# Triangle stage: channel sums kept in PSUM, squares summed on GpSimd, product stores on SyncE's queue, and the output stage's first tiles asked for earlier

## The chip, the cores and the metric

The kernel runs on one core of one Trainium2 chip. A core has five engines that run side by side, each with its own queue of instructions: PE (TensorE, matmuls), DVE (VectorE), ACT (ScalarE), POOL (GpSimd) and SP (SyncE, which here only issues transfers). They meet through semaphores. Transfers between the device's DRAM and the on-chip memory SBUF are issued on a queue (here SP's or POOL's) and carried out by 16 DMA engines. Matmuls write PSUM[...]. The metric is the device time of one execution in microseconds, as the median over several runs.

## The reference

Four residual layers on an image of 256 x 256 pixels with 128 channels, in float32. The change lies in the third, a gated triangle product:

```python
def _L2_conv_ref(pair, ln_in_w, ln_in_b, p_in_w, g_in_w, ln_out_w, ln_out_b, p_out_w, g_out_w):
    pair_norm = layer_norm(pair, ln_in_w, ln_in_b)
    p = jnp.einsum('bijd,hd->bijh', pair_norm, p_in_w)
    g = jax.nn.sigmoid(jnp.einsum('bijd,hd->bijh', pair_norm, g_in_w))
    left = g[..., :H] * p[..., :H]
    right = g[..., H:] * p[..., H:]
    out = jnp.einsum('bikd,bjkd->bijd', left, right / jnp.float32(L))
    out = layer_norm(out, ln_out_w, ln_out_b)
    out = jnp.einsum('bijh,dh->bijd', out, p_out_w)
    gate = jax.nn.sigmoid(jnp.einsum('bijd,ed->bije', pair_norm, g_out_w))
    return gate * out

x = x + _L2_conv_ref(_gn(x), ...)      # third of four such lines
```

For each of the 128 channels `d` the product is a 256 x 256 matrix, left times the transpose of right. The second layer norm runs over the channels, so it needs, for each pixel, the sum over the 128 products and the sum of their squares.

## The kernel before

`triangle` has three parts, run one after the other.

The first part normalises the image in tiles of 2048 pixels, keeps the result in DRAM as `znT`, keeps the inverse roots of its variances as `rs2D`, and already fills `LR` for the first quarter of the channels. `LR` is a tile of 128 KB per partition that holds left and right for 32 channels.

The second part is a loop over the four quarters `g`. A **fill** (not for `g` = 0) goes through the pixels in 64 blocks `b`: SP fetches `zt` from `znT`, 1 MB for two blocks, into `X[0]` to `X[3]` in turn; PE computes `z`, the gate and the value for 8 groups of 128 pixels, into two banks of PSUM; ACT takes the sigmoid of its first half (`sg`); DVE multiplies into `LR`. A **product stage** then goes through the 32 channels `d`: PE computes `po`, a product, in one bank of a `z` tile; ACT copies it, reordered and scaled, into `o` (two instructions); `o` is stored as a row of `prodD`; DVE forms `df`, the product less the first product (`shift`); the channel sum `total` is increased by `df` on DVE; and one product later, `add_square` has ACT square `df` and adds the square on POOL to `even`, or for every fourth channel on DVE to `odd`. `shift`, `total`, `even` and `odd` are the four quarters of the fifth tile, `X[4]`.

After the last quarter the sums are joined, ACT takes Ln and Exp of the variance (which need one table of functions, the sigmoid needs another; `table` asks for one), and the inverse roots go to DRAM as `rs3D`. In between, `transformed_taps` (called as `prepare`) makes the last layer's weights `U` from small matmuls `cpk`, ACT copies `kw` and a dozen short DVE instructions; its instructions may be placed among the others.

The third part, the output stage, goes through the image again in 32 tiles of 2048 pixels, with an order of steps written out by hand in `order`: `lx` and `lp` fetch `x` and the products `pd`; `pa` and `pb` spread the inverse roots `ra` (from `rs2D`) and `rb` (from `rs3D`) over the partitions by matmul; `xs` and `sc` scale; `e0` and `e1` give the gate `pe`, `y0` and `y1` the projected product `py`; `gy`, `ad`, `qu` and `st` finish a tile and store it. `ra` and `rb` are fetched by `roots`, four transfers for four tiles. `x` and `pd` have five buffers each.

Instructions wrapped in `pin` keep the order of the program on their engine. The others, among them SP's fetches, are placed by a scheduler. Memory comes from pools: a new tile that lies where an old one lay waits for the old one's last users. The tiles of the output stage lie where `X`, `LR` and the work tiles lay. Two engines that read the same PSUM tile are kept one behind the other, so `df` waits for `o`.

Of the kernel before, what the change touches and what calls it, by code (L numbers as in the profile page):

```python
# [9 lines left out]
F32 = mybir.dt.float32  # L10
AF = mybir.ActivationFunctionType
ALU = mybir.AluOpType
# [19 lines left out]
class Kernel:  # L32
# [21 lines left out]
    def act(self, out, in_, func, bias=0.0, scale=1.0, **kw):  # L54
        return self.nc.scalar.activation(out, in_, func, bias=bias, scale=scale, **kw)  # L55
# [4 lines left out]
    def mm(self, out, lhsT, rhs, start=True, stop=True):  # L60
        return self.nc.tensor.matmul(out, lhsT, rhs, start=start, stop=stop)  # L61
# [1050 lines left out]
    def triangle(self, x2T, x3T, znT, prodD, rs2D, rs3D, stats2, shift2, stats3, shift3, prepare):  # L1112
# [12 lines left out]
        with ExitStack() as c:  # L1125
# [70 lines left out]
            with ExitStack() as c1:  # L1196
# [97 lines left out]
                io = c1.enter_context(self.pool(name="t2", bufs=3))  # L1294
                ps = c1.enter_context(self.pool(name="t2s", bufs=2, space=PSUM))
                table(SIGMOID)
                shift, total, even, odd = (X[4][:, k * 512:(k + 1) * 512] for k in range(4))
                nc.gpsimd.memset(X[4][:, 512:], 0.0)
                squared = []

                def add_square():
                    if squared:
                        n, t = squared.pop()
                        act(t, t, AF.Square)
                        if n % 4:
                            pin(nc.gpsimd.tensor_tensor)(even, even, t, ADD)
                        else:
                            tt(odd, odd, t, ADD)

                for g in range(G):  # L1310

                    for b in range(NB if g else 0):
                        if b % 2 == 0:
                            zt = X[b // 2 % 4]
                            nc.sync.dma_start(zt, znT[:, b * 1024:(b + 2) * 1024])
                        z = ps.tile([P, 8, P], F32, name="z", bufs=4)
                        for ch in range(8):
                            o = (b % 2) * 1024 + ch * P
                            mm(z[:, ch, :], zt[:, o:o + P], wf[:, g].rearrange("c t d -> c (t d)"))
                        sg = work.tile([P, 8, 2 * CQ], F32, name="sg")  # L1320
                        act(sg, z[:, :, :2 * CQ], AF.Sigmoid)
                        rows = lambda t: t.rearrange("p (x q) f -> p x q f", x=2)
                        tt(LR[:, :, :, :, 2 * b:2 * b + 2].rearrange("p a k f x -> p x (a k) f"),
                           rows(z[:, :, 2 * CQ:]), rows(sg), MUL)

                    for d in range(CQ):
                        po = ps.tile([P, 8, P], F32, name="z", bufs=4)[:, :4]
                        pa = po.rearrange("p (a b) j -> p a b j", a=2)
                        for a in range(2):
                            for kc in range(2):  # L1330
                                mm(pa[:, a], LR[:, a, kc, d, :], LR[:, :, kc, CQ + d, :], start=kc == 0, stop=kc == 1)
                        o = io.tile([P, 2, P, 2], F32, name="o")
                        for a in range(2):
                            act(o[:, a], pa[:, a].rearrange("p b j -> p j b"), AF.Copy, scale=1.0 / N)
                        nc.gpsimd.dma_start(prodD[g * CQ + d].rearrange("(p a j) -> p a j", p=P, a=2),  # L1335
                                            o.rearrange("p a j b -> p a (j b)"))
                        add_square()
                        if g + d == 0:
                            act(shift, po.rearrange("p k j -> p (k j)"), AF.Copy, scale=1.0 / N)
                        else:  # L1340
                            df = io.tile([P, 512], F32, name="df", bufs=3)
                            stt(df, po.rearrange("p k j -> p (k j)"), 1.0 / N, shift, MUL, ALU.subtract)
                            tt(total, total, df, ADD)
                            squared.append((g * CQ + d, df))

                add_square()
                tt(even, even, odd, ADD)
                stt(total, total, -1.0 / P, total, MUL, MUL)
                tt(even, even, total, ADD)
                table(LN_EXP)  # L1350
                act(even, even, AF.Ln, bias=self.eps, scale=1.0 / P)
                rsm = io.tile([P, 2, P, 2], F32, name="o")
                for a in range(2):
                    act(rsm[:, a], even.rearrange("p (a b j) -> p a b j", a=2, b=2)[:, a].rearrange("p b j -> p j b"), AF.Exp, scale=-0.5)
                nc.sync.dma_start(rs3D[0].rearrange("(p n) -> p n", p=P), rsm.rearrange("p a j b -> p (a j b)"))

            quarters.close()
            prepare(W["kt"], W["wd"], W["bv"])
# [2 lines left out]
            with ExitStack() as c1:  # L1361
# [3 lines left out]
                D = [{} for _ in range(M)]  # L1365
                half = lambda t, h: t[:, h * 1024:(h + 1) * 1024]
                R = {}
                table(SIGMOID)

                def roots(b, name, src, queue=nc.sync):  # L1370
                    if b * 4 < M:
# [24 lines left out]
                load_x, load_pd = load("x", x2T, 5), load("pd", prodD, 5)  # L1396

                def lx(d):
                    if d["p"] % 4 == 0:
                        roots(d["p"] // 4 + 1, "ra", rs2D)  # L1400
                    load_x(d)

                def lp(d):
                    if d["p"] % 4 == 2:
# [39 lines left out]

                def st(d): pin(nc.gpsimd.dma_start)(x3T[:, d["p"] * 2048:(d["p"] + 1) * 2048], d["x"])

                roots(0, "ra", rs2D)
                roots(0, "rb", rs3D, nc.gpsimd)
                order = (
                     (lx, 0), (pa, 0), (y0, 1), (y1, 1), (xs, 0), (lp, 0), (gy, 1), (e0, 0), (pb, 0), (ad, 1),  # L1450
# [290 lines left out]
```

## Time and profile before

The three runs took 4733.85, 4735.3 and 4738.4 us; the median is 4735.3.

| | |
|---|---|
| profiled execution, its own time | 4734.2 us |
| its span (first to last instruction) | 4732.1 us |
| busy share PE, DVE, ACT, POOL | 96%, 80%, 70%, 45% |
| mean granted clock of PE | 0.989 |
| first part of `triangle` ends, first product | 3270.6 us |
| product stages on PE, first product to next stage's start | 59.2, 60.6, 60.6, 60.4 us |
| fills (three), 1024 matmul records each | about 115 us each |
| last product ends on PE, first `py` of the output stage | 3863.1, 3898.9 us |
| output stage, last layer | to 4195, to 4732 us |

In a line of the timeline the columns are the start in us from the span's start, the length in us, the engine, the line of the kernel, the instruction with its output and inputs, shapes and count; the bracket tells how long the engine had been idle before and what ended that wait. Consecutive equal instructions are merged. A line that belongs to a helper (55, 61, 1119) stands for every caller, so tiles tell more than lines. Each float32 matmul of the program shows as two records. `X`'s tiles, `shift`, `total`, `even` and `odd` are all named `zt` in the profile, and `po` is named `z`. SPq and POOLq are the queues' own issue times. In the list of groups the columns after the first bar are busy time in us and mean ns of one, after the second idle time before the group and what ended it.

### The profile page before, as it was taken

Reading aid. Unit: us, or ns where it says so; the run is one execution under the profiler, and the core shown is the slowest. Engines: PE = TensorE matmul, PEld = TensorE weight load, DVE = VectorE, ACT = ScalarE, POOL = GpSimd, SP = SyncE. Lnnn points to the kernel's source line nnn. Section 1 sums busy time; section 2 is a strip of 40 time slices with the busy share of each in tenths; the row PEclk is TensorE's granted clock in tenths of the full one; section 3 lists DMA queues with packets and bytes.
Section 4 is the critical chain, followed back from the end, with each engine's and each line's share of the span. In section 5 each row is a group of like instructions: output and inputs, shape, how many; then the busy total and the mean of one; then the engine's idle time right before and its main releaser. Section 6 shows DMA issues by size and latency. Waiting matters only on the chain.

```text
span 4732.1 us, 79416 instructions
## 1 busy us (share of the span) xinstructions
PE 4533.6 (96%) x30421; PEld 2596.8 (55%) x30421; DVE 3791.8 (80%) x4847; ACT 3332.4 (70%) x5174; POOL 2139.1 (45%) x1457
## 2 busy tenths in 40 slices
PE   8999999999999999999999998799999979999999
PEld 2444555555555533333333333456989963379999
DVE  6776777777777689999999999687676677789885
ACT  6555888888888899999999999697344344442210
POOL 0343555555555557666766666334142145520000
PEclk9999999999999999999999999899999989999999
DMA  8893122222222235555555555665756739955332
GB/s 305 301 349 140 46 84 88 82 85 81 90 81 86 81 87 134 132 131 130 135 131 130 135 131 116 206 260 216 267 208 238 264 138 344 362 218 172 127 118 72
DMA packets 212969, 769.13 MB, mean 163 GB/s; under 512 B 58630, under 2 KB 61980, under 8 KB 172244
## 3 DMA queue, kind: packets, MB, share of 16 engines
q1 hardware_dynamic: 136286, 432.10, 27.5%
q0 software_dynamic: 75008, 331.54, 23.8%
q8 instruction: 243, 3.98, 0.3%
q14 instruction: 136, 1.11, 0.1%
q10 hardware_dynamic: 1296, 0.40, 0.0%
HBM read 431.26 MB, written 265.55 MB: 147 GB/s over the span
## 4 chain that ended last, share of the span: by engine, by line
PE 61%; ACT 16%; DVE 12%; issue 7%; DMA 2%; POOL 1%; SPq 0%; ACTq 0%; POOLq 0%; DVEq 0%
PE z L61 10%; PE m L61 8%; PE nd L61 7%; PE sc L61 6%; PE ppq L61 3%; PE ppv L61 3%; PE pe L61 2%; PE zc L61 2%; PE py L61 2%; PE ppg L61 2%; PE ppk L61 2%; PE px L61 2%; ACT L933 2%; PE pr L61 2%; ACT x2q L55 2%
## 5 line engine op out<-in xcount | busy, mean ns | idle before, releaser
L592 DVE TENSOR_TENSOR e<-sc,bT 128x1024 f32<-128x1024 f32 x512 | 613.1, 1219 | 256.1 <-PE sc L61 254.0
L592 POOL TENSOR_TENSOR ks<-e 128x1024 f32<-128x1024 f32 x256 | 601.6, 2370 | 442.7 <-PE nd L61 429.3
L55 ACT ACTIVATE e<-e 128x1024 f32<-128x1024 f32 x512 | 539.0, 1053 | 39.2 <-DVE e L592 29.6
L61 PE MATMUL m<-U,v 128*128 128x128 f32 x4608 | 514.8, 275 | 0.0
L61 PEld LDWEIGHTS m<-U,v 128*128 128x128 f32 x4608 | 514.6, 192 | 0.0
L61 PEld LDWEIGHTS z<-wf,zt 128*128 128x128 f32 x4096 | 462.8, 192 | 55.7 <-DVE LR L1119 27.4
L61 PE MATMUL z<-wf,zt 128*128 128x128 f32 x4096 | 475.5, 277 | 7.2 <-DVE LR L1119 4.9
L1119 DVE TENSOR_TENSOR LR<-z,sg 128x512 f32<-128x512 f32 (+1 forms) x320 | 268.3, 873 | 156.9 <-ACT sg L55 156.9
L55 ACT ACTIVATE sg<-z 128x512 f32<-128x512 f32 (+1 forms) x320 | 159.8, 512 | 233.7 <-PE z L61 230.2
L61 PE MATMUL sc<-proj 32*128 32x256 f32 x4096 | 299.9, 403 | 3.1 <-DVE e L592 2.2
L961 POOL TENSOR_TENSOR fs<-f 128x512 f32<-128x512 f32 x64 | 175.7, 2746 | 269.8 <-DVE f L958 250.2
L61 PEld LDWEIGHTS sc<-proj 32*128 32x128 f32 x4096 | 187.9, 185 | 160.8 <-PE px L61 94.8
L61 PE MATMUL nd<-e,proj 128*32 128x256 f32 x4096 | 272.3, 384 | 2.6 <-DVE og L592 2.6
L61 PE MATMUL z<-LR 128*128 128x256 f32 x1024 | 226.6, 381 | 21.4 <-DVE df L1119 15.1
L55 ACT ACTIVATE dn<-dn 128x512 f32<-128x512 f32 x384 | 237.9, 620 | 10.3 <-DVE dn L592 6.2
L961 POOL TENSOR_TENSOR u<-t,tr 128x512 f32<-128x512 f32 x64 | 235.3, 3677 | 11.8 <-DVE tr L964 10.6
L961 POOL TENSOR_TENSOR t<-t,v 128x1024 f32<-128x1024 f32 x64 | 210.2, 3284 | 57.3 <-DVE t L958 57.3
L1335 POOL DMA_DIRECT2D prodD<-o x128 | 70.7, 553 | 356.4 <-ACT o L55 352.9
L1626 POOL DMA_DIRECT2D out_dram<-ys x32 | 37.0, 1155 | 424.0 <-DVE ys L1624 412.1
L61 PEld LDWEIGHTS z<-LR 128*128 128x128 f32 x1024 | 192.5, 190 | 54.7 <-issue 21.0
L1616 ACT COPY m4s<-m 128x512 f32<-128x512 f32 x32 | 18.6, 583 | 287.3 <-PE m L61 287.3
L1119 POOL TENSOR_TENSOR x<-ga,x 128x1024 f32<-128x1024 f32 x62 | 144.6, 2347 | 135.6 <-DVE ga L1119 135.6
(408 smaller groups left out, 10920.8 us busy)
## 6 DMA issues: line engine op xcount, KB each, us to landing
zt<-znT SPq DMA_DIRECT2D x96, 1024.0 KB
xin<-in_x_dram SPq DMA_DIRECT2D x48, 1024.0 KB
xr<-x3T SPq DMA_DIRECT2D x46, 768.0 KB
x1T<-x POOLq DMA_DIRECT2D x64, 512.0 KB, 4.9
xf<-x1T SPq DMA_DIRECT2D x64, 512.0 KB
xc<-x1T SPq DMA_DIRECT2D x128, 256.0 KB
xc<-t POOLq DMA_DIRECT2D x64, 512.0 KB, 4.7
xc<-yf POOLq DMA_DIRECT2D x64, 512.0 KB, 5.0
```

What stands on the lines that cost most here:

```text
L55: return self.nc.scalar.activation(out, in_, func, bias=bias, scale=scale, **kw)
L61: return self.nc.tensor.matmul(out, lhsT, rhs, start=start, stop=stop)
L592: pin = lambda f: lambda *a, **k: tc.keep_in_program_order(f(*a, **k))
L933: pin(nc.scalar.preload_act_table_set(want))
L961: pin(nc.gpsimd.tensor_tensor(out, a, b_, op))
L1119: pin = lambda f: lambda *a, **k: tc.keep_in_program_order(f(*a, **k))
L1335: nc.gpsimd.dma_start(prodD[g * CQ + d].rearrange("(p a j) -> p a j", p=P, a=2), o.rearrange("p a j b -> p a (j b)"))
L1616: nc.scalar.copy(m4, m[4])
L1626: nc.gpsimd.dma_start(out[row:row + 8].rearrange("r p t c -> p (r t) c"), ys.rearrange("p g k t c -> p (g k t) c"))
```

## The change

The channel sums move from `total` in SBUF to `sums`, a tile of one bank in PSUM; `z` has three buffers in place of four. All squares are added on POOL, into one sum, which now has the name `total`; `odd` is gone. The stores of the products are issued by SP. The first four fetches of a fill are written ahead of the previous product stage. In a fill's last block the sigmoid and the multiplication into `LR` are each done in two halves. At the end ACT squares the channel sums, and one subtraction joins them with the sum of squares; the table for the sigmoid is asked for behind the last Exp. `rs3D` is stored by POOL. The output stage's first four `x` are asked for before its loop, its first `ra` is fetched by POOL, and each later `ra` one turn later than before.

```diff
-                shift, total, even, odd = (X[4][:, k * 512:(k + 1) * 512] for k in range(4))
-                nc.gpsimd.memset(X[4][:, 512:], 0.0)
-                squared = []
+                shift, total, v = (X[4][:, k * 512:(k + 1) * 512] for k in range(3))
+                sums = ps.tile([P, 512], F32, name="sums", bufs=1)
+                V.memset(sums, 0.0)
+                nc.gpsimd.memset(total, 0.0)
+                squared, zt = [], {}
 
                 def add_square():
                     if squared:
-                        n, t = squared.pop()
+                        t = squared.pop()
                         act(t, t, AF.Square)
-                        if n % 4:
-                            pin(nc.gpsimd.tensor_tensor)(even, even, t, ADD)
-                        else:
-                            tt(odd, odd, t, ADD)
+                        pin(nc.gpsimd.tensor_tensor)(total, total, t, ADD)
+
+                def fetch(g, n):
+                    if g < G:
+                        zt[g, n] = X[n % 4]
+                        nc.sync.dma_start(zt[g, n], znT[:, n * 2048:(n + 1) * 2048])
 
                 for g in range(G):
                     for b in range(NB if g else 0):
-                        if b % 2 == 0:
-                            zt = X[b // 2 % 4]
-                            nc.sync.dma_start(zt, znT[:, b * 1024:(b + 2) * 1024])
-                        z = ps.tile([P, 8, P], F32, name="z", bufs=4)
+                        if b % 2 == 0 and b >= 8:
+                            fetch(g, b // 2)
+                        z = ps.tile([P, 8, P], F32, name="z", bufs=3)
...
-                        act(sg, z[:, :, :2 * CQ], AF.Sigmoid)
-                        rows = lambda t: t.rearrange("p (x q) f -> p x q f", x=2)
-                        tt(LR[:, :, :, :, 2 * b:2 * b + 2].rearrange("p a k f x -> p x (a k) f"),
-                           rows(z[:, :, 2 * CQ:]), rows(sg), MUL)
+                        rows = lambda t: t.rearrange("p (x q) f -> p x q f", q=4)
+                        for x, w in ((0, 2),) if b < NB - 1 else ((0, 1), (1, 1)):
+                            c = slice(4 * x, 4 * (x + w))
+                            act(sg[:, c], z[:, c, :2 * CQ], AF.Sigmoid)
+                            tt(LR[:, :, :, :, 2 * b + x:2 * b + x + w].rearrange("p a k f x -> p x (a k) f"),
+                               rows(z[:, c, 2 * CQ:]), rows(sg[:, c]), MUL)
+
+                    for n in range(4):
+                        fetch(g + 1, n)
                     for d in range(CQ):
-                        po = ps.tile([P, 8, P], F32, name="z", bufs=4)[:, :4]
+                        po = ps.tile([P, 8, P], F32, name="z", bufs=3)[:, :4]
...
-                        nc.gpsimd.dma_start(prodD[g * CQ + d].rearrange("(p a j) -> p a j", p=P, a=2),
-                                            o.rearrange("p a j b -> p a (j b)"))
+                        nc.sync.dma_start(prodD[g * CQ + d].rearrange("(p a j) -> p a j", p=P, a=2),
+                                          o.rearrange("p a j b -> p a (j b)"))
...
-                            tt(total, total, df, ADD)
-                            squared.append((g * CQ + d, df))
+                            tt(sums, sums, df, ADD)
+                            squared.append(df)
 
                 add_square()
-                tt(even, even, odd, ADD)
-                stt(total, total, -1.0 / P, total, MUL, MUL)
-                tt(even, even, total, ADD)
+                act(v, sums, AF.Square, scale=1.0 / math.sqrt(P))
                 table(LN_EXP)
-                act(even, even, AF.Ln, bias=self.eps, scale=1.0 / P)
+                tt(total, total, v, ALU.subtract)
+                act(total, total, AF.Ln, bias=self.eps, scale=1.0 / P)
...
-                    act(rsm[:, a], even.rearrange(...), AF.Exp, scale=-0.5)
-                nc.sync.dma_start(rs3D[0].rearrange("(p n) -> p n", p=P), rsm.rearrange("p a j b -> p (a j b)"))
+                    last = act(rsm[:, a], total.rearrange(...), AF.Exp, scale=-0.5)
+                self.chain("roots", last)
+                nc.gpsimd.dma_start(rs3D[0].rearrange("(p n) -> p n", p=P), rsm.rearrange("p a j b -> p (a j b)"))
...
-                table(SIGMOID)
+                self.chain("roots", table(SIGMOID))
...
                 def lx(d):
-                    if d["p"] % 4 == 0:
+                    if d["p"] % 4 == 1:
                         roots(d["p"] // 4 + 1, "ra", rs2D)
-                    load_x(d)
+                    if d["p"] > 3:
+                        load_x(d)
...
-                roots(0, "ra", rs2D)
+                for p in range(4):
+                    D[p]["p"] = p
+                    load_x(D[p])
+                roots(0, "ra", rs2D, nc.gpsimd)
                 roots(0, "rb", rs3D, nc.gpsimd)
```

`chain` ties two instructions of a key in program order.

More of the change, by code (lines that the diff above doesn't have):

```diff
@@ L1317, in triangle @@
                         for ch in range(8):
                             o = (b % 2) * 1024 + ch * P
-                            mm(z[:, ch, :], zt[:, o:o + P], wf[:, g].rearrange("c t d -> c (t d)"))
+                            mm(z[:, ch, :], zt[g, b // 2][:, o:o + P], wf[:, g].rearrange("c t d -> c (t d)"))
                         sg = work.tile([P, 8, 2 * CQ], F32, name="sg")
-                        act(sg, z[:, :, :2 * CQ], AF.Sigmoid)
-                        rows = lambda t: t.rearrange("p (x q) f -> p x q f", x=2)
@@ L1342, in triangle @@
                             stt(df, po.rearrange("p k j -> p (k j)"), 1.0 / N, shift, MUL, ALU.subtract)
-                            tt(total, total, df, ADD)
-                            squared.append((g * CQ + d, df))
+                            tt(sums, sums, df, ADD)
+                            squared.append(df)
                 add_square()
-                tt(even, even, odd, ADD)
-                stt(total, total, -1.0 / P, total, MUL, MUL)
-                tt(even, even, total, ADD)
+                act(v, sums, AF.Square, scale=1.0 / math.sqrt(P))
                 table(LN_EXP)
-                act(even, even, AF.Ln, bias=self.eps, scale=1.0 / P)
+                tt(total, total, v, ALU.subtract)
+                act(total, total, AF.Ln, bias=self.eps, scale=1.0 / P)
                 rsm = io.tile([P, 2, P, 2], F32, name="o")
                 for a in range(2):
-                    act(rsm[:, a], even.rearrange("p (a b j) -> p a b j", a=2, b=2)[:, a].rearrange("p b j -> p j b"), AF.Exp, scale=-0.5)
-                nc.sync.dma_start(rs3D[0].rearrange("(p n) -> p n", p=P), rsm.rearrange("p a j b -> p (a j b)"))
+                    last = act(rsm[:, a], total.rearrange("p (a b j) -> p a b j", a=2, b=2)[:, a].rearrange("p b j -> p j b"), AF.Exp, scale=-0.5)
+                self.chain("roots", last)
+                nc.gpsimd.dma_start(rs3D[0].rearrange("(p n) -> p n", p=P), rsm.rearrange("p a j b -> p (a j b)"))
             quarters.close()
```

## The prediction

> **What bounds the kernel now.** I read the busy shares first: PE is busy 96% of the span, so a gain has to come from the places where PE waits. Reading on by stage, the columns fill, product, fill, product ... of `triangle` lie between 3270 and 3863 us, the output stage from about 3889 to 4195. The fills are PE's own (a chain piece of 1008 matmul records takes 112.8 us without a gap). The product stages are not. PE's timeline for the third of them:
>
> ```profile
> 3624.91 22.71 PE L61 MATMUL z<-LR 128*128 128x256 f32 x104 [1.74 <-DVE LR L1119]
> ...
> 3664.31 7.14 PE L61 MATMUL z<-LR 128*128 128x256 f32 x32 [0.80 <-DVE df L1119]
> 3672.25 7.14 PE L61 MATMUL z<-LR 128*128 128x256 f32 x32 [0.80 <-DVE df L1119]
> ...
> 3688.17 2.02 PE L61 MATMUL z<-wf,zt 128*128 128x128 f32 x16 [0.75 <-DVE df L1119]
> ```
>
> Each start, length, engine, tile; in brackets the idle time before it. At the start PE waits 1.74 us for the last LR; it then runs 13 products freely on the four buffers; from there it stops 0.8 us in every four products (8 records each) until DVE has read a `z`. The last stop falls into the next fill. Four products take 7.95 us (3664.31 to 3672.25), 1.99 each. What fills DVE's 1.99:
>
> ```profile
> L1119 DVE TENSOR_TENSOR zt<-zt,df 128x512 f32<-128x512 f32 x36 | 33.7, 936 | 6.3 <-ACT df L55 5.3
> L1119 POOL TENSOR_TENSOR zt<-zt,df 128x512 f32<-128x512 f32 x21 | 29.1, 1385 | 12.1 <-ACT df L55 11.8
> L1119 DVE SCALAR_TENSOR_TENSOR df<-z,zt 128x512 f32<-128x512 f32 x29 | 19.8, 683 | 2.8 <-ACT o L55 2.8
> ...
> L1335 POOL DMA_DIRECT2D prodD<-o x28 | 15.5, 553 | 114.5 <-ACT o L55 114.3 <-issue 0.2
> ```
>
> These are the groups of one product stage. DVE does one `df` (0.683) and 1.25 adds per product (0.936 mean), and every fourth add sits idle for 0.76 until ACT has squared. The add is not one price:
>
> ```profile
> 3850.03 0.69 DVE L1119 TENSOR_TENSOR zt<-zt,df 128x512 f32<-128x512 f32 x1
> ...
> 3854.36 1.18 DVE L1119 TENSOR_TENSOR zt<-zt,df 128x512 f32<-128x512 f32 x1
> ...
> 3855.49 1.28 POOL L1119 TENSOR_TENSOR zt<-zt,df 128x512 f32<-128x512 f32 x1
> ```
>
> 0.69 alone, 1.18 when it starts while POOL adds (the one from 3853.70). Then the hand-over to the output stage:
>
> ```profile
> 3869.68 2.62 POOL L1119 TENSOR_TENSOR zt<-zt,df 128x512 f32<-128x512 f32 x2
> ...
> 3875.13 1.28 ACT L1119 ACT_TABLE_LOAD   x1
> 3876.42 1.28 ACT L55 ACT_TABLE_LOAD   x1
> ...
> 3878.58 0.33 SPq L1355 DMA_DIRECT2D rs3D<-o  x1
> 3878.99 4.89 SPq L1375 DMA_DIRECT2D ra<-rs2D  x8
> ...
> 3883.99 0.39 SPq L1393 DMA_DIRECT2D x<-x2T  x1
> ...
> 3889.43 2.47 DVE L1119 SCALAR_TENSOR_TENSOR xs<-x,shift,ra 128x1024 f32<-128x1024 f32 x2 [10.19 <-DMA x<-x2T]
> ...
> 3898.89 3.70 PE L61 MATMUL py<-pd,two 128*128 128x512 f32 x8
> ```
>
> Call T the end of the last product on PE (3863.1). POOL's sums end at T+9; two table loads stand between Ln and Exp; SP stands at `rs3D` until T+15.5, issues eight `ra`, and only at T+20.9 the first `x`. It lands at 3889.3, and the first `py` starts at T+35.8. From there every turn takes 9.40 us, PE 98% busy, so each us by which that `py` comes earlier reaches the end.
>
> [...] `df`, which has one PSUM input, stays at 0.68 beside POOL. [...] No row here has DVE writing PSUM. [...] `x` landed 5.3 us after its issue, the pair `pd` behind it about 4 later. [...]
>
> **The change, part by part.**
>
> *Channel sums in PSUM, squares on POOL.* DVE per product: `df` 0.72 start to start, and one add from PSUM and SBUF to PSUM. Price not in the trace: below, 0.69 (the free add); above, 1.91 (the longest add row); I take 0.75, because only one input is in SBUF. 1.47 in all. The wait for ACT's square goes. POOL: one add per product, 1.28 (up to 1.59), and no DMA issue. ACT is unchanged, two `o` in 0.66 and a square of 0.63. So PE is the longest: (22.31 - 0.19) / 103 = 0.215 us between weight loads in its free run, 256 x 0.215 = 55.0 per stage, 1.72 per product. `sums` takes a bank, so `z` has three buffers: `df` starts after `o` (it waits for it now as well) and ends 0.1 + 0.66 + 0.72 = 1.5 after PE, while PE needs the buffer 3.4 after. In the fills a `z` is held 1.79 + 0.6 + 1.05 + waits = 3.7 of 5.4. Both free; the cover is 1.7 us.
> Now, from the first product to where the fill would have begun unstalled (start of its 17th record less 16 x 0.112): 60.1, 61.5, 61.5, and 60.4 to `cpb` in the last. Less 55.0 each: 5.1 + 6.5 + 6.5 + 5.4 = **23.5 us**. If the start of each stage costs more, 18; if PE keeps 0.2133 between weight loads, its rate in the pieces of 32, 25.
>
> *Stores on SP.* 128 issues leave POOL (0.553 each) and join SP (about 0.35 for such an issue). Behind them on SP stand the later `znT` fetches: the fifth is due 3.6 us after the fill begins, the last store about 1 us after the products end. The first stores stand behind the last 1 MB fetch: that ends about 5.3 after the fill, store 0 is issued at 3.7 and lands near 6.6, and `o` number 3, which needs its buffer, is due at 8.0. Nothing, with 1.4 us of cover; without it 1 us per stage. The four prefetches stand as early as before.
>
> *Last block in halves.* Three stages: the final sigmoid 0.38 for 0.60, the final LR 0.58 for 1.04; 0.64 each, **1.9 us** (0.5 to 2.2). Three more instructions on ACT and DVE each lie under the fill.
>
> *Memsets.* DVE's of `sums` follows the last LR at 3270.6, `df` first runs at 3275.1: nothing, 4 us of cover. POOL's is shorter.
>
> *Hand-over.* In the built order SP has last store, four `x`, two parts of `pd`, four `ra`. The four `x` do not come during the products: they stand behind the last store, and the second lies in the memory of X[4], waits for the last Exp and holds the others. POOL has `rs3D`, four `ra`, four `rb`. By T: `o` T+0.75, last `df` 1.5, sums 2.3, last square 2.2, its square of the sums 3.0, table load 4.3; POOL's last two adds 3.9; subtraction 4.7, Ln 5.4, one `kw` copy that now stands before Exp 5.9, Exp 6.8. The reload to sigmoid comes after. `rs3D` on POOL 6.8, landed 9.6; `ra` issued to 9.5 (0.51 each as `rb` has), landed 11.8; `rb` issued 9.6 to 11.7, landed 14. DVE's twelve tap instructions (5.0 us, once hidden under the load of `x`) need the second `kw` copy and run 7.3 to 12.3; `xs` from 12.4, `pe` from 13.9 and slow (3.78, as before, where the granted clock of 3886 to 3894 was 0.50), `rb` 17.7, second `pe` and next `ra` to 22.3. First `x` issued T+1.4, landed 6.7. Second `x` issued 6.8; it, two more and `pd` are 4 MB in a row, 2 + 4 x 3.3 = T+22 (3.3 per MB from the 2 MB that took about 9 us to land). `sc` then 1.2, `py` at T+23.4, against 35.8: **12.4 us**. What ends last is `pd`, PE 1 us behind. With `pd` at once, T+21 to 22; with loads 3 us slower, T+26.5: 9 to 15. Moving each later `ra` by one turn costs nothing: it is used three turns on.
>
> Sum: 23.5 + 1.9 + 12.4 = 37.8. The profiled execution took 4734.2 (span 4732.1), so 4696.4; the median of the runs is 1.1 above it: **4697.5**. By the ends, 18 + 0.5 + 9 to 25 + 2.2 + 15 is 27 to 42: 4693 to 4708.
>
> **Rivals.**
> *DVE stays the bound (slower from one price on).* With the add in PSUM at p, DVE needs 0.72 + p per product; above p = 1.0 it outlasts PE, and 128 x (p - 1.0) eats the gain. At 1.2 about 12 us are left (4723); at 1.295 nothing; at 1.45 the kernel is 20 us slower (4755), at the longest add row, 1.91, 79 (4814). Against it: `pd<-pd,rb`, with one PSUM input, takes 1.21 to 1.22 for 1024 elements in all its 64 rows, POOL busy or not. For it: reading and writing one bank in one instruction is nowhere in the trace.
> *The hand-over gives little.* `pd` arrives at T+29 because loads, `rb` and `ra` crowd the DMA engines: 7 instead of 12, 4703. Speaks for it: `pd` now stands behind four `x`, earlier behind one.
> *A new wait on the stores.* If SP's stores land 3 us later than POOL's (median 2.3), ACT waits for `o` and the products run at 1.85: 128 x 0.13 = 17 lost, 4714.
> *The change does not do what it says:* with `x` not asked for early, as read above; it is in the figure. Were it early, PE would end last and `py` start at T+22.3: 4696.
>
> **How the numbers follow.** Likeliest 0.74 (4693 to 4708); small hand-over 0.08; stores 0.06; DVE at p of 1.0 to 1.22 0.07 (4698 to 4726), at 1.22 to 1.37 0.02, above 0.03. A difference of 0.2% (9.5 us) is about what a measurement of this kernel can tell from none. Faster (below 4726) is the sum of the first four less a rest, 0.93; same 0.03; slower 0.04. The range, 4692 to 4714, takes in the likeliest, the small hand-over and the nearer half of the stores and DVE cases.
>
> **What would show it.** Right: product stages of 55 to 56 us, no wait of PE for `df` in them, the DVE add at 0.7 to 0.8 whatever POOL does; 1.1 us before each first product; POOL adds 127 x 1.28; no table load between Ln and Exp; `py` about 23 us after the last product, released through `pd`. Wrong: the add over 1.0, PE waiting for `df` or ACT for a store, or `py` later than T+27.

## The result, and the profile after

The changed kernel takes 4711.0 us (median of five runs, 4710.96 to 4713.07) against 4735.5 before (five runs): a ratio of 0.9949, 95% interval 0.9934 to 0.9964. That is 24.4 us less, where 37.8 was predicted (4697.5); the range, 4692 to 4714, holds it. The profiled executions differ by 21.1 (4713.1 against 4734.2), and on these the ledger is made. T is the end of the last product on PE, 3847.34 us in the changed kernel and 3863.5 before. (The 3863.1 of the prediction is where the last weight load ends; its T lies 0.4 earlier.)

| | before | after | gained | predicted |
|---|---|---|---|---|
| first product to T | 592.9 | 574.9 | 18.0 | 25.4 |
| T to the first `py` | 35.4 | 32.5 | 2.9 | 12.4 |
| both | 628.3 | 607.4 | 20.9 | 37.8 |

The first product starts 1.8 us later than before, in a part that the change does not touch, and the stretch after `py` is 1.9 shorter; these cancel.

**The product stages** are PE's now. The groups of the third stage (busy time and mean ns of one, then idle time before the group):

```profile
L61 PE MATMUL z<-LR 128*128 128x256 f32 x256 | 57.2, 387 | 2.1 <-DVE LR L1119 2.1
...
L1119 POOL TENSOR_TENSOR zt<-zt,df 128x512 f32<-128x512 f32 x31 | 39.4, 1269 | 132.6 <-ACT df L55 132.6
L1119 DVE TENSOR_TENSOR sums<-sums,df 128x512 f32<-128x512 f32 x31 | 21.7, 699 | 1.1
L1119 DVE SCALAR_TENSOR_TENSOR df<-z,zt 128x512 f32<-128x512 f32 x31 | 21.4, 692 | 13.6 <-ACT o L55 13.6
```

PE's only wait is the one ahead of the first product. The add in PSUM takes 0.70 us (0.699 to 0.700 in all 127), DVE is busy for 1.39 of each 1.73 us, POOL for 1.27. But that first wait grew from 1.74 to 2.13, and the stage is 57.0 long, not 55. The timeline of the last block of the second stage's fill:

```profile
3442.35 0.39 ACT L55 ACTIVATE sg<-z 128x256 f32<-128x256 f32 x1 [1.19 <-PE z L61]
3442.77 0.59 DVE L1119 TENSOR_TENSOR LR<-z,sg 128x256 f32<-128x256 f32 x1 [0.52 <-ACT sg L55]
3443.39 0.38 ACT L55 ACTIVATE sg<-z 128x256 f32<-128x256 f32 x1 [0.65 <-DVE LR L1119]
3443.81 0.59 DVE L1119 TENSOR_TENSOR LR<-z,sg 128x256 f32<-128x256 f32 x1 [0.45 <-ACT sg L55]
...
3444.45 3.78 PE L61 MATMUL z<-LR 128*128 128x256 f32 x10 [2.13 <-DVE LR L1119]
```

The first half waits for the whole `z`, and the second sigmoid for the first half's multiplication: four instructions in a row in place of two. What follows is shown by the windows behind it (length, then busy time and count of PE, its weight loads, DVE, ACT and POOL, then PE's granted clock, the DMA engines' share and GB/s):

```profile
3446.00:3448.00 2.00, 2.00 (x6) 1.56 (x5) 0.00 (x0) 0.58 (x3) 0.00 (x0) 0.50 0.19 78
3448.00:3450.00 2.00, 2.00 (x9) 1.70 (x8) 1.39 (x2) 0.70 (x3) 1.26 (x1) 0.81 0.35 131
```

Six matmul records in 2 us where nine or ten belong: PE's granted clock is at half (0.50) for 3.41 us, from 3445.36 to 3448.77.

**The hand-over**, in the timeline (SPq is the issue on SP's queue):

```profile
3848.53 7.08 SPq L1400 DMA_DIRECT2D x<-x2T  x4
...
3854.61 0.59 POOL L1362 DMA_DIRECT2D rs3D<-o  x1 [2.87 <-ACT o L55]
...
3855.19 2.05 POOL L1382 DMA_DIRECT2D ra<-rs2D  x4
...
3855.70 1.15 SPq L1400 DMA_DIRECT2D pd<-prodD  x2
...
3862.00 1.50 POOL L1382 DMA_DIRECT2D rb<-rs3D  x3 [4.76 <-DMA rs3D<-o]
...
3862.77 3.69 PE L61 MATMUL ra<-ra,tones 1*128 1x512 f32 x8 [7.59 <-DMA ra<-rs2D]
...
3866.61 3.75 PE L61 MATMUL pe<-xs,twe 128*128 128x512 f32 x4 [0.15 <-DVE xs L1119]
...
3870.30 4.84 PE L61 MATMUL rb<-rb,tones 1*128 1x512 f32 x8
...
3879.86 3.70 PE L61 MATMUL py<-pd,two 128*128 128x512 f32 x8
```

The chain up to the issue of `rs3D` and `ra` runs as forecast, within half a us: both are on their way by T+9.9. There it stops. The list of transfers between 3846 and 3885 gives the median time from issue to landing in the last column:

```profile
rs3D<-o POOLq DMA_DIRECT2D x1, 256.0 KB, 7.1
ra<-rs2D POOLq DMA_DIRECT2D x4, 8.0 KB, 7.4
...
rb<-rs3D POOLq DMA_DIRECT2D x4, 8.0 KB, 8.2
```

In the kernel before, `rb` landed 1.9 us after its issue. Now three small transfers, two of them one behind the other, take 7 to 8 us each beside the 4 MB of `x` and `pd` that SP has just issued (the DMA engines are at 1.0 from 3858 to 3870). And PE's granted clock is at half (0.50) from 3858.4 to 3878.9 (in the kernel before, from 3867.9 to 3895.3).

### The profile page after: what moved, and what is told of

Read it like the earlier page. It is cut to its first block, busy times and chain, and to the rows that moved or that the text cites. A ratio compares the mean times of both kernels' runs of the same rounds, so it can differ in the third digit from the quotient of the medians.

```text
span 4711.2 us, 79401 instructions
## 1 busy us (share of the span) xinstructions
PE 4538.0 (96%) x30421; PEld 2602.1 (55%) x30421; DVE 3746.5 (80%) x4818; ACT 3332.6 (71%) x5176; POOL 2104.2 (45%) x1365
## 4 chain that ended last, share of the span: by engine, by line
PE 65%; ACT 15%; DVE 11%; issue 6%; DMA 2%; POOL 1%; SPq 0%; ACTq 0%; POOLq 0%; DVEq 0%
PE z L61 14%; PE m L61 8%; PE nd L61 7%; PE sc L61 6%; PE ppq L61 3%; PE ppv L61 3%; PE pe L61 3%; PE zc L61 2%; PE py L61 2%; PE ppg L61 2%; PE ppk L61 2%; PE px L61 2%; ACT L933 2%; PE pr L61 2%; ACT x2q L55 2%
## 5 line engine op out<-in xcount | busy, mean ns | idle before, releaser
L1119 POOL TENSOR_TENSOR zt<-zt,df 128x512 f32<-128x512 f32 x127 | 161.5, 1272 | 422.8 <-ACT df L55 422.6
```

Of the source, the lines that this page charges most:

```text
L1119: pin = lambda f: lambda *a, **k: tc.keep_in_program_order(f(*a, **k))
```

## The experiments

All times below are profiled, with T and `py` as above. Where the first turn of the output stage was longer than the regular 9.40 us, `py` is put back from a later one by 9.40 a turn. The parts before `triangle` move a kernel's start by up to 9 us from one execution to the next, so these two stretches say more than a median of four or five runs; medians and ratios to the kernel before stand beside them.

| kernel | first product to T | T to `py` | median | ratio, 95% interval |
|---|---|---|---|---|
| before | 592.9 | 35.4 | 4735.5 | |
| changed | 574.9 | 32.5 | 4711.0 | 0.9949 (0.9934 to 0.9964) |
| whole block | 570.3 | 36.8 | 4708.2 | 0.9937 (0.9918 to 0.9956) |
| matmuls in the gap | 571.6 | 36.0 | 4710.1 | 0.9946 (0.9932 to 0.9959) |
| stores on POOL | 574.9 | 34.0 | 4714.6 | 0.9952 (0.9937 to 0.9966) |
| sums in SBUF | 574.9 | 32.8 | 4715.9 | 0.9956 (0.9940 to 0.9973) |
| three `x` behind `rb` | 574.9 | 33.4 | 4712.4 | 0.9949 (0.9930 to 0.9968) |
| PE busy behind `cpk` | 576.5 | 29.6 | 4714.0 | 0.9953 (0.9937 to 0.9968) |
| PE busy from T on | 574.9 | 36.6 | 4712.7 | 0.9949 (0.9932 to 0.9966) |
| busy, new order | 576.6 | 23.5 | 4708.3 | 0.9940 (0.9924 to 0.9957) |
| new order alone | 574.9 | 22.2 | 4703.7 | 0.9935 (0.9920 to 0.9950) |
| busy, order, whole block | 570.3 | 22.4 | 4700.5 | 0.9933 (0.9916 to 0.9950) |
| own tiles, order, busy | 568.4 | 21.5 | 4696.3 | 0.9918 (0.9905 to 0.9932) |
| own tiles and order | 568.4 | 22.0 | 4701.3 | 0.9917 (0.9904 to 0.9931) |

### The start of a stage: the last block in one piece

```diff
-                        for x, w in ((0, 2),) if b < NB - 1 else ((0, 1), (1, 1)):
+                        for x, w in ((0, 2),):
```

> One edit to the changed kernel: the last block of each fill is done in one piece again. Theory: the two halves run one behind the other (sigmoid, multiplication, sigmoid, multiplication, 0.39 + 0.59 twice and their waits), so the wait before a stage's first product falls back from 2.13 to about 1.74 us; and the longer gap is what lets PE's clock fall to half for some 3.5 us at the start of the second and third stage, so these stages take 55.4 instead of 57.0. In all 3 x 0.4 + 2 x 1.65 = 4.5 us less, 4706.5. Rival: the clock's fall has nothing to do with the gap; then only 1.2 us, 4709.8, and the two stages stay at 57. A second rival is the prediction itself: the split is worth 1.9, and this kernel is slower, 4713.

PE's timeline at the start of the second stage, and the window over it:

```profile
3446.54 2.64 PE L61 MATMUL z<-LR 128*128 128x256 f32 x11 [1.73 <-DVE LR L1119]
```

```profile
3446.50:3448.50 2.00, 1.96 (x9) 1.75 (x10) 0.00 (x0) 0.00 (x0) 0.00 (x0) 1.00 0.94 381
```

The wait is back at 1.73, the clock stays at 1.00, and the four stages take 55.4, 55.4, 55.4 and 55.5. From first product to T 4.6 us are saved, as the theory said: 3 x 0.4 of waiting and two falls of the clock of 1.7 each. The hand-over of this execution, the same program as in the changed kernel, happened to be 4.3 us longer, its clock at half until 3885.

### Is it the idle time? Eight matmuls in the gap

```diff
+                    for _ in range(8 if g else 0):
+                        mm(idle, self.ident, self.cmat)
                     for n in range(4):
                         fetch(g + 1, n)
```

(`idle` has a bank of its own.)

> One edit to the changed kernel: between the last z of a fill and the stage's first product PE does eight matmuls without use, about 1.7 of the 2.13 us for which it waits. Nothing else is sooner. Theory: PE's clock falls at the start of a stage because PE has stood idle for 2.13 us; with some 0.4 us of idle time left the second to fourth stage take 55.4 each, none 57.0: about 3 x 0.76 x 1.68 = 4 us less than the changed kernel (16 of the 21 stages behind a gap of 2.13 us seen so far took 57.0). Rival: the fall comes from the split block's instructions or from chance; then two or three of the stages still take 57.0.

```profile
3439.12 1.95 PE L61 MATMUL idle<-cmat,ident 128*128 128x128 f32 x16
3441.43 4.80 PE L61 MATMUL z<-LR 128*128 128x256 f32 x21 [0.36 <-DVE LR L1119]
```

LR comes as late as in the changed kernel; PE only does not stand idle. All stages take 55.4, and first product to T is 3.3 us shorter: the fall of the clock comes from the gap. Over the profiled runs of all kernels, 18 of 24 stages behind a gap of 2.13 us began with it, none of 18 behind 0.36 to 1.74 (the kernel before among them).

The six that did not fall are no chance either. In every trace the granted clock changes only on a fixed grid: within one execution, all falls to half clock lie whole steps of 3.41 us apart, and each lasts whole steps (but for the one that the end of the trace cuts off). Here is the step with the gap and the step behind it, for two stages of the changed kernel (columns as in the windows above):

```profile
3441.95:3445.36 3.41, 1.27 (x8) 1.01 (x7) 1.47 (x3) 0.77 (x2) 0.00 (x0) 1.00 0.81 281
3445.36:3448.77 3.41, 3.41 (x10) 2.68 (x9) 0.61 (x1) 1.18 (x3) 0.03 (x1) 0.50 0.30 127
...
3790.11:3793.52 3.41, 1.70 (x8) 1.52 (x9) 1.18 (x2) 0.38 (x1) 0.00 (x0) 1.00 0.00 0
3793.52:3796.94 3.42, 3.42 (x18) 3.01 (x17) 2.00 (x3) 2.35 (x6) 1.31 (x2) 1.00 0.20 77
```

In the 18 stages that began at half clock, at least 2.09 us of the gap lay inside one step. In the other six an edge of the grid cut the gap, and at most 1.89 us lay inside one. So a gap of 2.13 us is a matter of where it falls, and one of 1.74 is below that wherever it falls.

### Stores back on POOL

```diff
-                        nc.sync.dma_start(prodD[g * CQ + d].rearrange("(p a j) -> p a j", p=P, a=2),
+                        nc.gpsimd.dma_start(prodD[g * CQ + d].rearrange("(p a j) -> p a j", p=P, a=2),
```

> One edit to the changed kernel: the products are stored from POOL's queue again. Theory: POOL then has 1.27 (add) and 0.55 (issue) = 1.82 us per product, more than PE's 1.73, and df has three buffers, which give about 1.1 us of slack; so each stage loses 32 x 0.09 - 1.1 = 1.8 us, and POOL's sum ends about 1 us later in the hand-over: 8 us slower, 4719, with DVE's df waiting for POOL late in each stage. Rival: POOL's issues fit beside its adds, the stages stay at 55.5 and 57, and the time stays within 2 us of 4711. If SP's stores were what delays the first x at the hand-over, this kernel would also start the output stage sooner.

Groups of the third stage:

```profile
L1119 POOL TENSOR_TENSOR zt<-zt,df 128x512 f32<-128x512 f32 x29 | 37.3, 1285 | 0.6
L1119 DVE SCALAR_TENSOR_TENSOR df<-z,zt 128x512 f32<-128x512 f32 x31 | 21.4, 692 | 14.0 <-ACT o L55 11.2 <-POOL zt L1119 2.8
...
L1342 POOL DMA_DIRECT2D prodD<-o x30 | 16.7, 557 | 116.0 <-ACT o L55 116.0
```

POOL is full (1.285 + 0.557 = 1.84 us per product against PE's 1.73), and DVE and ACT do wait for it. Yet no stage is longer: presumably the buffers of `df`, `o` and `z` absorb the 32 x 0.11 us, and the fill lets POOL catch up. What is left is POOL's last sum, `cpb` at T+4.7 instead of T+3.5, and `py` 1.5 later. Between the two expectations: the stages as the rival, a small loss behind T as the theory. Nor had SP's stores held back the first `x`: it is issued at T+9.5 here, at T+1.2 in the changed kernel. The move to SP is worth a us or two here, and room for POOL.

### Channel sums in SBUF again

```diff
-                sums = ps.tile([P, 512], F32, name="sums", bufs=1)
-                shift, total, v = (X[4][:, k * 512:(k + 1) * 512] for k in range(3))
+                shift, total, v, sums = (X[4][:, k * 512:(k + 1) * 512] for k in range(4))
```

> One edit to the changed kernel: the channel sums lie in SBUF (the free quarter of X[4]) instead of PSUM; squares stay on POOL. Theory: [...] DVE's add takes 1.2 to 1.9 as in the kernel before, DVE needs 1.9 to 2.6 us per product, and the four stages are 128 x 0.2 to 0.9 = 25 to 110 us longer; I take 40, 4750. Rival: the add slips into the 0.45 us in which POOL is free, stays at 0.7 to 0.9, and the stages stay at 55 to 57: then the gain came from taking the squares off DVE, and PSUM brought nothing.

Groups of the third stage; the sums are among the `zt`:

```profile
L1119 POOL TENSOR_TENSOR zt<-zt,df 128x512 f32<-128x512 f32 x30 | 48.5, 1617 | 120.1 <-ACT df L55 117.9
L1119 DVE TENSOR_TENSOR zt<-zt,df 128x512 f32<-128x512 f32 x31 | 25.0, 805 | 1.1
```

The theory falls. The stages are 55.4, 57.0, 55.4 and 57.2, as with PSUM. With the sums in SBUF both adds take longer, but POOL pays: its add takes 1.62 instead of 1.27, DVE's 0.81 instead of 0.70, and both still fit into 1.73. What freed the stages, by elimination, is that DVE no longer adds squares and no longer waits for ACT; no run gives the squares back to DVE. With the stores on SP, PSUM gave POOL room and took nothing off the path. PSUM and the move of the stores both relieve POOL, and each was taken back alone: with both taken back, POOL would need some 1.62 + 0.56 = 2.18 us per product against PE's 1.73 (an estimate from these two runs), which no run tried.

### The hand-over: three x behind rb

```diff
                 for p in range(4):
                     D[p]["p"] = p
-                    load_x(D[p])
+                load_x(D[0])
                 roots(0, "ra", rs2D, nc.gpsimd)
                 roots(0, "rb", rs3D, nc.gpsimd)
+                for p in range(1, 4):
+                    load_x(D[p], nc.gpsimd)
```

> One edit to the changed kernel: only the first x is asked for ahead; the next three are issued by POOL, behind the first rb, and so after rs3D has landed. Theory: in the changed kernel rs3D, ra and rb take 7 to 8 us each because they share the DMA engines with 4 MB of x and pd; without those three x in front they land in 2.5 to 4, ra at T+12.5 and rb at T+16 (T: end of the last product), and the first py starts at T+27 to 28 instead of T+32.5: about 5 us less, 4706. Rival: PE at half clock decides (pe 3.75 us twice, rb 4.8), the small transfers being early changes little: py at T+30 to 31, 4709.5. Second rival: x1 to x3 then come too late for the second to fourth turns, which wait for them as long as was gained: 4711 or more.

```profile
3850.34 1.79 SPq L1400 DMA_DIRECT2D pd<-prodD  x2
...
3851.87 0.58 POOL L1362 DMA_DIRECT2D rs3D<-o  x1 [2.88 <-ACT o L55]
...
3860.92 1.49 POOL L1382 DMA_DIRECT2D rb<-rs3D  x3 [6.34 <-DMA rs3D<-o]
```

The edit did not clear the way. The `x` had held SP's queue; with them gone, the `pd` of the second turn was issued ahead of `rs3D`, so 3 MB were still issued in front of it and `rs3D` took 8.8 us. But three of the four `rb` behind it landed 2.1 to 2.4 us after their issue, the third at T+19.7, where it was T+24.2 in the changed kernel; `py` still came no earlier, while PE's clock was at half from T+4.6 to T+35.3. That speaks for the first rival, PE's clock. The second rival is out: from the second `py` on, the turns take 9.40 us.

### The hand-over: PE kept at work

Behind `cpk` only, and then from T on:

```diff
                 roots(0, "ra", rs2D, nc.gpsimd)
+                idle = ps.tile([P, 1024], F32, name="idle", tag="w")
+                for _ in range(36):
+                    mm(idle[:, :P], self.ident, self.cmat)
```

> One edit to the changed kernel: 36 matmuls without use follow the last cpk on PE, about 7.7 us at full clock, up to where the ra matmuls begin. Theory: PE's clock falls to half because PE stands idle for 8 us, and this costs the hand-over: with PE kept at work the two pe take 1.9 instead of 3.75 us, and py starts about 3 us earlier, at T+29.5, held by rb's landing (T+25.7) rather than by PE: 4708. Rival: the clock falls all the same, or rb's transfer ends last anyway and takes up the gain: py at T+32, 4711.

```diff
+                for _ in range(16):
+                    mm(idle, self.ident, self.cmat)
                 add_square()
                 act(v, sums, AF.Square, scale=1.0 / math.sqrt(P))
...
             prepare(W["kt"], W["wd"], W["bv"])
+            for _ in range(28):
+                mm(idle, self.ident, self.cmat)
...
```

> One edit to the changed kernel: 16 matmuls without use stand on PE directly behind the last product (3.5 us, where it waited for a bank) and 28 behind the last cpk (6 us), in a bank of their own. Counted with T, the end of the last product, and with the first py put back from the regular turns behind it by 9.40 us each. Theory: the granted clock falls in the first 3.5 us without work and comes back only after many us of work, so PE must be kept at work from T on; then ra, both pe and rb run at full clock, rb's landing at T+25.7 decides, and py starts at T+28 to 29 instead of T+32.5. Rival: the clock falls whatever PE does (the work without use does not count, or DMA load lowers it): py at T+32 to 33. Second rival: only one of the two gaps matters; then no better than the T+29.6 of the kernel with matmuls in the second gap alone.

In the changed kernel PE waits 3.52 us behind T and 7.59 us for `ra`. Its clock is at half from 3851.55 to 3854.96 and again from 3858.37 to 3878.85, though from 3862.77 on PE is at work.

Windows of the first kernel, then of the second:

```profile
3862.00:3866.00 4.00, 4.00 (x34) 4.00 (x33) 0.00 (x0) 0.00 (x0) 2.00 (x4) 0.89 1.07 377
3866.00:3870.00 4.00, 3.07 (x26) 2.12 (x25) 0.87 (x1) 0.00 (x0) 0.00 (x0) 1.00 1.03 228
```

```profile
3858.00:3862.00 4.00, 1.15 (x9) 0.86 (x8) 0.00 (x0) 0.00 (x0) 1.05 (x3) 1.00 1.02 416
...
3866.00:3870.00 4.00, 4.00 (x6) 1.53 (x6) 0.74 (x1) 0.83 (x1) 0.00 (x0) 0.50 1.04 222
```

In the first, the matmuls without use run on past the landing of `ra` (T+17.1) to T+20.4; the clock is full for `pe` and `rb`, and `py` starts at T+29.6, as expected. In the second they end at T+13.5, PE waits 2.85 us for `ra`, the clock falls and stays at half until about 3884: T+36.6, which no theory had. The last `rb` landed at T+25.5 in the first and at T+27.0 in the second, so most of the 7 us between them is the clock.

The grid shows why the clock stays at half while PE is at work. Steps of the second kernel, and what PE did in them:

```profile
3869.07 5.18 PE L61 MATMUL rb<-rb,tones 1*128 1x512 f32 x8
...
3870.02:3873.43 3.41, 3.41 (x8) 1.11 (x5) 1.22 (x1) 0.27 (x1) 0.00 (x0) 0.50 0.44 109
...
3879.91 5.55 PE L61 MATMUL py<-pd,two 128*128 128x512 f32 x8
...
3880.26:3883.67 3.41, 3.41 (x5) 1.34 (x5) 2.23 (x2) 0.00 (x0) 0.00 (x0) 0.50 1.03 437
3883.67:3887.08 3.41, 3.41 (x9) 1.24 (x7) 2.59 (x4) 0.00 (x0) 1.90 (x1) 1.00 0.16 67
```

The first of these steps is filled with the matmuls of `rb`, which use one of 128 rows (`1*128`), and the clock stays at half behind it. The second is filled with `py`, which uses all 128, and behind it the clock is full. If only matmuls of 128 rows count as work, the steps between 3262 and 3900 us of all 14 profiled executions fit. At full clock, the next step was at half behind each of the 36 steps with at most 1.33 us of such work, and behind none of the others, which had 1.52 us or more. At half clock, it stayed at half behind all 55 steps with at most 2.69 us and came back behind all 33 with 3.05 us or more; the six between went either way. The load on the DMA engines does not decide: their share was 0.44 in the step that left the clock at half and 1.03 in the one that brought it back. No run changes `ra` or `rb` themselves, so this is read from the traces and not shown by an edit.

So read, the late transfers cost twice: as a wait (7.59 us for `ra` in the changed kernel), and by leaving PE without matmuls of 128 rows while its clock is at half (20.5 us there).

### The order of the transfers

```diff
-                for p in range(4):
+                for p in range(5):
                     D[p]["p"] = p
-                    load_x(D[p])
-                roots(0, "ra", rs2D, nc.gpsimd)
+                roots(0, "ra", rs2D)
+                load_x(D[0])
+                load_pd(D[0])
                 roots(0, "rb", rs3D, nc.gpsimd)
+                for p in range(1, 5):
+                    load_x(D[p], nc.gpsimd)
+                    load_pd(D[p], nc.gpsimd)
```

Without a queue named, SP issues; POOL's stand behind `rs3D` and `rb`. (The steps `lx` and `lp` leave out the first five turns.) First with PE kept at work:

> The kernel before this one, with the transfers of the hand-over in another order: SP issues the first ra, then the first x and pd; POOL issues rs3D, rb, and behind rb x and pd of the next four turns. Theory: the small transfers are late because they share the DMA engines with 4 MB of x and pd. Then ra lands near T+6, rs3D takes under 4 us, rb lands near T+14; xs waits for DVE's tap instructions (to T+12.5 or 13), pe starts near T+14, and py at T+20 to 21: 12 us earlier than in the changed kernel, 4698 to 4700. Rival: a small transfer takes 7 us anyhow: rb lands at T+21, py at T+25. Second rival: the later x and pd are now too late, and the second to fourth turns give back what the first gained.

`py` at T+23.5, 9.0 us earlier than in the changed kernel and some 3 short of the expectation: `rs3D` still took 7.2 us behind 2 MB of `x` and `pd`. Then alone:

> The new order of the transfers alone, on the changed kernel, with no matmuls without use. py counted as before (T, and back from the regular turns). Theory: order and clock both count, and each hides the other's gain. With the order alone ra and rb land as early as in the kernel with both (rb at about T+18), but PE runs at half clock: both pe, rb and ra take 5.5 us more, and py starts at T+27 to 29, against T+32.5 to 36.8 in the changed kernel's order and T+22.5 to 23.7 with both. Rival: the order does all of it, py at T+23 to 24. Second rival: the clock does all of it, py at T+32 or later.

```profile
3846.46 2.46 SPq L1382 DMA_DIRECT2D ra<-rs2D  x4
...
3852.54 0.59 POOL L1362 DMA_DIRECT2D rs3D<-o  x1 [2.88 <-ACT o L55]
...
3859.54 3.67 PE L61 MATMUL pe<-xs,twe 128*128 128x512 f32 x4 [4.13 <-DVE xs L1119]
3859.82 2.04 POOL L1382 DMA_DIRECT2D rb<-rs3D  x4 [6.69 <-DVE xs L1119]
...
3863.14 1.43 PE L61 MATMUL rb<-rb,tones 1*128 1x512 f32 x8
...
3867.49 2.84 PE L61 MATMUL py<-pd,two 128*128 128x512 f32 x6
```

Here T is 3845.28, and `py` starts at T+22.2: the rival is right, in this execution the order does all of it. `ra` is there before DVE's tap instructions end, `rb` takes 2.0 us with nothing large under way (the DMA engines are at 0.10 from 3858 to 3862), and the one slow `pe` lies beside `rb`'s transfer. I had expected half clock through the whole turn; it ended at T+17.7. In part that is luck: this `pe` began within 0.02 us of an edge of the clock's grid and filled the step, so the clock was full from `rb` on.

### Together

The new order, PE kept at work, and the last block in one piece:

> The changed kernel with the last block of a fill in one piece, PE kept at work in the hand-over and the transfers in the new order: the three edits together. Theory: they add up, 4.5 us from the whole block and the clock it keeps, about 12 from the hand-over: 4694 to 4696, stages of 55.4, py at T+20 to 21. Rival: what the hand-over gains is given back in the first turns, or shares its cause with the first edit (PE's clock): 4700 or more.

The gains add up (570.3 and T+22.4); the time is 4700.5, 5 above the expectation, `py` being 2 later than I had put it and the rest no more than what such medians scatter. Then with halves that are independent, and the first `x` ahead of `ra` and the first `pd` behind `rs3D`:

```diff
-                        z = ps.tile([P, 8, P], F32, name="z", bufs=3)
-                        for ch in range(8):
-                            o = (b % 2) * 1024 + ch * P
-                            mm(z[:, ch, :], zt[g, b // 2][:, o:o + P], wf[:, g].rearrange("c t d -> c (t d)"))
-                        sg = work.tile([P, 8, 2 * CQ], F32, name="sg")
                         rows = lambda t: t.rearrange("p (x q) f -> p x q f", q=4)
                         for x, w in ((0, 2),) if b < NB - 1 else ((0, 1), (1, 1)):
                             c = slice(4 * x, 4 * (x + w))
+                            z = ps.tile([P, 8, P], F32, name="z", bufs=3)
+                            sg = work.tile([P, 8, 2 * CQ], F32, name="sg")
+                            for ch in range(4 * x, 4 * (x + w)):
+                                o = (b % 2) * 1024 + ch * P
+                                mm(z[:, ch, :], zt[g, b // 2][:, o:o + P], wf[:, g].rearrange("c t d -> c (t d)"))
...
```

> The kernel with the three edits together, with two changes: the two halves of a fill's last block get z and sg tiles of their own, so that neither waits for the other, and the first x is issued ahead of ra, the first pd by POOL behind rs3D, with 18 instead of 28 matmuls without use behind cpk. Theory: the wait before a first product is 1.1 us, as in the first stage, 0.64 less in three stages; rs3D no longer stands behind 1 MB of pd, lands in some 4 us and rb at T+15, so py starts at T+20: 2 + 2.5 us less than with the three edits, 4696. Rival: rb is as late as before, behind pd on POOL's queue, and only the 2 us come: 4698.5. Second rival: pd ends last now, py at T+23 or later, 4699 or more.

> The best kernel so far without its matmuls without use: halves with tiles of their own and the new order of transfers, nothing else, on the changed kernel. Theory: the matmuls without use are not needed, since the order alone gave py at T+22.2; here the first pe falls into a half clock of PE (3.7 instead of 3.3 us), py at T+21.5 to 22.5, and the time is 4696 to 4697.5, the same as with them (4696.3). Rival: without them PE's idle times of 3.5 and 4 us keep its clock at half through the first turn, py at T+25 or later, 4700.

In both the gap is the 1.1 us that the prediction gave to the split. From the second of the two, PE's timeline at a stage's start, and the transfers of its hand-over:

```profile
3439.89 2.43 PE L61 MATMUL z<-LR 128*128 128x256 f32 x10 [1.09 <-DVE LR L1119]
```

```profile
rs3D<-o POOLq DMA_DIRECT2D x1, 256.0 KB, 2.4
...
rb<-rs3D POOLq DMA_DIRECT2D x4, 8.0 KB, 4.6
```

`rs3D` lands in 2.4 us at last, but then `rb` meets the first part of `pd` and takes 4.6, and `xs` starts only when DVE is done with the taps, at T+13. So `py` stays at T+22: the expected 2.5 us did not come, the 2 from the halves did. The two ratios are 0.9918 and 0.9917 (4696.3 and 4701.3 us, against 4735.1 and 4738.6 for the kernel before beside them), so they show no use of the matmuls without use. But that is not settled: the profiled execution without them took 4694.3 us and its first `pe` again met an edge of the grid, within 0.02 us, while three of the five executions took 4701 to 4702, with a mean clock of 0.991 in place of 0.993. Both kernels beat the changed one; their intervals lie just below its own.

## Why the prediction was right and wrong

**Products: right, 18.9 of 23.5.** DVE's add in PSUM was priced 0.75, my estimate on top of the free add's 0.69, and is 0.70, whatever POOL does; PE is the bound, and none of the waits for `df` is left. The stages took 55.4, 57.0, 57.0 and 55.5 us, against 60.1, 61.5, 61.5 and 60.8, the last counted to T. They are 55.4 where nothing disturbs them, not 55.0, because PE takes 0.216 us from weight load to weight load, in the trace before as well; the 0.215 came from a row in which one load followed the other early. That is 1.6 us over four stages. Another 3.4 are two falls of the clock, which the sum did not have; 0.4 come back because the prediction's T lay early. One of its reasons was beside the point: the 1.18 us adds of DVE under POOL were no reason why the sums had to leave SBUF, since with every square on POOL it is mostly POOL's adds that get longer there (1.62 us instead of 1.27; DVE's 0.81 instead of 0.70).

**The last block in halves: wrong in sign, -1.2 instead of +1.9.** The step that failed is "the final sigmoid 0.38 for 0.60, the final LR 0.58 for 1.04". It took the two halves as independent, but they share one `z` and one `sg`. With a tile each the gap is 1.10 and the 1.9 us are there. The lengthened gap is also what set off the clock's falls, so this edit cost 4.6 in this execution.

**Stores: right at nothing.** ACT waits for no store. (That SP's transfers land in the order of their issue was my assumption in this step, not shown by a run.) The move mattered on the other side: with the stores on POOL, POOL is full.

**Hand-over: the chain was right, the term for the transfers was not; 2.9 instead of 12.4.** The table load, the Exp, the second `x` held by X[4] until T+7 and the burst behind it all came as written. What failed is "landed 9.6" for `rs3D`, "landed 11.8" for `ra` and "landed 14" for `rb`: durations of 2.3 to 2.8 us, from rows in which no large transfer was under way, used in the same paragraph that put 4 MB on the DMA engines at the same moment. Measured: T+14.4, T+15.3 to 17.0, T+25.7. I had charged the burst to `pd` alone and let `pd` end last; the small ones on the other queue ended last. The rival "the hand-over gives little" named the crowding by `rb` and `ra`, but again with `pd` as the victim and 7 us as what is left. `py` later than T+27 was named as what would show the step wrong.

Nor did POOL's transfers of 8 KB slip in between SP's megabytes: `ra` and `rb` took 7.4 and 8.2 us, where `rb` took 1.9 in the kernel before. As to the clock, a fall lasts 3.41 us at the start of a stage, and whole steps of 3.41 us throughout. A gap of 2.13 us was enough for one in 18 of 24 cases, those with 2.09 us or more inside one step. And the hand-over stayed at half for 20.5 us on end in the changed kernel, and for 30.7 with three `x` behind `rb`, though PE had work in much of it. The grid and the one-row matmuls of `ra` and `rb` fit that in every trace, as read above.

With the two failed steps mended, "own tiles and order" gains 24.5 up to T and 13.4 behind it, 37.9 in all in its profiled execution, against the 37.8 of the prediction: the places were right, the change as written does not reach them. That the time of the change as written still lies in the range is luck in part. The upper end, 4714, had been put there for late stores and a slower add, and neither came; what did come, a last block that cost time and falls of the clock, was in none of its cases.

## What to carry to other kernels

A landing time taken from a quiet stretch of a trace did not hold in a burst (1.9 us for `rb` in the kernel before, 8.2 in the changed one): when an edit starts a burst, charge it first to the small transfers on which a chain waits, on whatever queue, and issue those ahead of it. A step cut in halves gained only when each half had its own tiles (a gap of 1.1 us instead of 2.13), since the waits followed the tile and not the slice: on shared tiles the second sigmoid stood 0.65 us until the first half's multiplication was done. And look at the gap in front of a stage on PE not only for its length: with 2.09 us or more of it inside one step of the grid, it cost nearly as much again in clock here (1.7 us). Where PE did only one-row matmuls, its clock stayed as if it were idle (0.50 behind a step full of `rb`'s), so do not count that as work.

## What was not expected of the hardware

- The granted clock of PE changed only on a grid of 3.41 us. A gap of 2.13 us was followed by one step at 0.50 (1.7 us lost) when at least 2.09 us of it lay inside one step (18 of 24 cases), and not when an edge cut it (six, at most 1.89); gaps of 1.74 and less never were.
- Matmuls that use one of 128 rows did not count as work for the clock, as the 14 traces read: a step filled with `rb`'s left it at half (0.50), behind one filled with `py`'s it was full (1.00). No edit changed the rows.
- An 8 KB transfer took 7.4 to 8.2 us in the median beside a 4 MB burst on another queue (the DMA engines at 1.0), and 1.9 to 2.4 with nothing large under way (at 0.08 to 0.11 in the kernel before).
- DVE adding SBUF to PSUM in place, 128 x 512 float32, takes 0.70 us, as much as from SBUF to SBUF (0.69), and no more beside POOL (0.699 to 0.700 in all 127). With both in SBUF, DVE takes 0.81 and POOL's add 1.62 instead of 1.27: the delay fell mostly on POOL.
